# One half step of a windowed-attention transformer: its scores in one run, its value projections together at the end, the roots of the norms ahead of the softmax, and every softmax division on POOL

## The chip, the cores and the metric

The kernel runs on one core of a Trainium2 chip. The metric is the device time of one execution in microseconds (us). The engines are TensorE (PE in the profile; its weight loads are listed apart as PEld), VectorE (DVE), ScalarE (ACT), GpSimd (POOL) and SyncE (SP, which issues nearly all DMAs here). Each takes its instructions in the order in which they were written; semaphores tie the engines together.

## The reference, cut to what matters

The input is 16 sequences of 256 tokens with 128 features, all in float32. A first block adds one layer of causal attention. The second block, which takes most of the time and holds the whole change, runs six layers over the normed result. Cut to its core, with `x` of shape (16, 256, 128), 16 heads of 64 features, and windows of 32 tokens:

```python
def attn_layer(x, Wqkv, qs, ksc, Wo):
    q, k, v = split_heads(x @ Wqkv)            # 16 heads x 64
    q = l2norm(q) * qs                          # norm over the 64 features of a head
    k = l2norm(k) * ksc
    q = q * cos * scale + rotate_half(q) * sin * scale
    k = k * cos / scale + rotate_half(k) * sin / scale
    sim = einsum('bhwie,bhwje->bhwij', windows(q), look_back(windows(k))) * 8
    attn = softmax(where(mask, -max, sim))      # 32 queries x 64 keys (own window, one before)
    out = einsum('bhwij,bhwje->bhwie', attn, look_back(windows(v)))
    return merge_heads(out) @ Wo

for i in range(6):
    x = attn_layer(shift_tokens(x), Wqkv[i], q_scale[i], k_scale[i], Wo[i]) + x
    x = ffn_layer(shift_tokens(x), ln_g[i], ln_b[i], W1[i], b1[i], W2[i], b2[i]) + x
```

`shift_tokens` moves half of the features one token down. `ffn_layer` is a layer norm, two matrices of 128 x 341 with a gelu gate, and a matrix back.

## The kernel before, in words

The second block is a pipeline over `n`, which counts layer and sequence together (6 x 16 = 96 values). A step `n` has two halves, `half(n, 0)` and `half(n, 1)`. A half works at once on the scores of `n`, on the projections of `n + 2`, on the norms of `n + 1`, and on the values of the half before it: in `half(n, 0)` those of heads group `u = 1` of `n - 1`, in `half(n, 1)` those of `u = 0` of `n`. The gated feed-forward works on pairs of sequences, so that its pieces fall differently on even and odd `n`. Four kinds of half follow each other, 48 times: **A** is `half(even, 0)`, **B** `half(even, 1)`, **C** `half(odd, 0)`, **D** `half(odd, 1)`. In this text a half is counted from its first mask matmul, which is the last step but one of the written half before; the value projection that follows the masks (and, in C, the matmuls `w2` before it) is thus at the head of the counted half.

The order inside each half is written out by hand. A function `in_order` ties every instruction of PE, DVE, ACT and POOL to the one before it on its engine, so that these four run in the written order. SP's queue is not tied. The functions, in short, with their lines:

- `proj_qk` (L463 to L477): a group of q and k heads: matmuls into a PSUM tile `qk` (one for q, one for k); ACT squares it (L464); DVE multiplies it with the rotary tables into `t` (L465, 1024 elements wide, it waits for ACT on the same tile); POOL adds the squares (L474) and the two rotary products (L477, twice, into `tq`). A half does it for group i early, called `qk i` here, and for group j late, `qk j`, whose q part and k part stand apart on PE.
- `norms` (called by `sums`) and `roots`: matmuls sum the squares (L484), ACT copies them (L489), PE transposes them (`nT`, L495), and DVE makes the reciprocal roots with a shift trick and three Newton steps: L499, L503, then three times L506, L507, L508. POOL spreads the k part into `kb` (L511). Only halves A and C do this, for `n + 1`.
- `spread_k` and `norm_k`: PE transposes `kb` into PSUM (`bc`, L522), DVE scales the keys with it (L536), and eight DMAs per step move q and k into the layout of the scores (`us`, L538).
- `masks`, `sim`: the scores of one `u` on top of masks (L563, L583). One call of `sim` is one group of heads; a half makes four.
- `soften`: DVE scales the scores by the roots of q's norms (L595) and takes the row maximum (L603); POOL subtracts it (L604). Then `power` (exponential, ACT, L610) and, in the next half, `share`: DVE sums and inverts (L617, L618), and the division is a multiplication (L620).
- `attn_T`, `attn_v`, `project_out`: PE transposes the weights (`aT`, L626), ACT copies them (L628), PE multiplies them with v (`po`, L646), ACT copies (L655); in the next step the output matrix is applied (`wo`, L666), and DVE adds it to the residual (`yT`, L671).
- `proj_v`: two pieces, c = 0 and 1, each one matmul (L546), one ACT copy into `vn` (L552) and DMAs into `vs`, the copy of v that is shifted by one window: L553 for each piece, L555 for piece 0 alone.
- The feed-forward: `glu_center` (`cen`, L685), `glu_var` (`pv`, L696), `glu_norm` (`rs`, L708), `glu_part` (`hg` and `ha`, L728 and L729), `glu_out` (`w2`, L742).

PSUM has eight banks here: four for the scores and the value products (two tiles of two banks), and four for everything else, through `psum1`. So a `psum1` tile must wait until the last reader of the tile that held its bank before is done:

```python
ps_o = st.enter_context(tc.tile_pool(name="ps_o", bufs=4, space=PSUM))
ps_s = st.enter_context(tc.tile_pool(name="ps_s", bufs=2, space=PSUM))
```

Of the kernel before, what the change touches and what calls it, by code (L numbers as in the profile page):

```python
# [11 lines left out]
ALU = mybir.AluOpType  # L12
# [9 lines left out]
NG = HEADS // 4  # L22
# [16 lines left out]
def tile_transformer(  # L39
# [16 lines left out]
    nc = tc.nc  # L56
    P = 128
# [298 lines left out]
    with ExitStack() as st:  # L356
# [18 lines left out]
        def psum1(name):  # L375
            return ps_o.tile([P, 512], F32, tag="o", name=name)
# [115 lines left out]
        def roots(n, n2):  # L492
            ps = psum1(f"nT_{n}").rearrange("p (h g m) -> p h g m", h=4, g=4)
            for h in range(2):
                nc.tensor.transpose(  # L495
                    ps[:, h].rearrange("p g m -> p (g m)"), n2[:, h].rearrange("p a m -> p (a m)"), ident
                )
            x = p2.tile([P, 2, NG, 8], F32, tag="nx", name=f"nx_{n}")
            nc.vector.tensor_scalar(x, ps[:, 0:2, :, 0:8], 1e-24, None, ALU.max)  # L499

            y = p3.tile([P, 2, NG, 8], F32, tag="rn", name=f"rn_{n}")
            x_, y_ = (v.rearrange("p h g m -> p (h g m)") for v in (x, y))
            nc.vector.tensor_scalar(y_.bitcast(I32), x_.bitcast(I32), -0.5, 1597463007.0, ALU.mult, ALU.add)  # L503
            for _ in range(3):
                z = p4.tile([P, 64], F32, tag="nz", name=f"nz_{n}")
                nc.vector.tensor_tensor(z, x_, y_, ALU.mult)  # L506
                nc.vector.scalar_tensor_tensor(z, z, -0.5, y_, ALU.mult, ALU.mult)  # L507
                nc.vector.scalar_tensor_tensor(y_, z, 1.5, y_, ALU.add, ALU.mult)  # L508
            rn[n] = y
            kb = p1.tile([P, 2, NG, P], F32, tag="kb", name=f"kb_{n}")  # L510
            nc.gpsimd.tensor_copy(  # L511
                kb.rearrange("p h g (i d) -> p (h g) i d", d=32),
                y.rearrange("p h g m -> p (h g) m")[:, :, 4:8].unsqueeze(3).to_broadcast([P, 8, 4, 32]),
            )
            kbs[n] = kb
# [97 lines left out]
        def share(n, i):  # L613

            seg = exs[n, i].rearrange("p g (h k) -> p (g h) k", h=2)
            rec = p4.tile([P, 8], F32, tag="rec", name=f"rec_{n}_{i}")
            nc.vector.tensor_reduce(rec, seg, AX.X, ALU.add)  # L617
            nc.vector.reciprocal(rec, rec)  # L618
            on = nc.vector if i == 1 else nc.gpsimd
            on.tensor_tensor(seg, seg, rec.unsqueeze(2).to_broadcast([P, 8, 64]), ALU.mult)  # L620

        def attn_T(n, i):
            ex = exs.pop((n, i))
# [52 lines left out]
        def glu_shift(m):  # L676
            b = m % 8
            x2 = x2s[m] = p1.tile([P, 2 * S], F32, tag="gl", name=f"x2_{m}")
            for i in range(2):
                shifted(x2[:, i * S : (i + 1) * S], 2 * b + i)  # L680

        def glu_center(m):
            x2 = x2s.pop(m)
            ps = psum1(f"cen_{m}")
            nc.tensor.matmul(ps, center, x2, start=True, stop=True)  # L685
            sq2 = p1.tile([P, 2 * S], F32, tag="h1", name=f"fsq_{m}")
            nc.scalar.activation(sq2, ps, AF.Square)
            xc = p1.tile([P, 2 * S], F32, tag="h2", name=f"xc_{m}")
            nc.scalar.copy(xc, ps)
            xns[m] = sq2, xc  # L690
# [12 lines left out]
        def glu_norm(m):  # L703
            l = m // 8
            rstd, xc = xns[m]
            ps = psum1(f"rs_{m}")
            for t in range(4):
                nc.tensor.matmul(  # L708
                    ps[:, t * P : (t + 1) * P],
                    rstd[:, t : t + 1].to_broadcast([P, P]),  # L710
                    ident,
                    start=True,
                    stop=True,
                    is_transpose=True,
                )
            xn = p1.tile([P, 2 * S], F32, tag="xn", name=f"xn_{m}")
            nc.vector.tensor_tensor(xn, ps, xc, ALU.mult)
            nc.gpsimd.tensor_scalar(xn, xn, vecs[:, l, V_G : V_G + 1], vecs[:, l, V_B : V_B + 1], ALU.mult, ALU.add)
            xns[m] = xn

        def glu_part(mm, i):
            l = mm // 8
            if mm % 8 == 0 and i == 0:
                load_glu(l)
            xn = xns[mm]
            a, m = DI_PARTS[i]
            pg, ph = psum1(f"hg_{mm}_{i}"), psum1(f"ha_{mm}_{i}")
            nc.tensor.matmul(pg[:m], W["1"][:, DI + a : DI + a + m], xn, start=True, stop=True)  # L728
            nc.tensor.matmul(ph[:m], W["1"][:, a : a + m], xn, start=True, stop=True)  # L729
            g = p1.tile([P, 2 * S], F32, tag="gl", name=f"g_{mm}_{i}")  # L730
            nc.scalar.activation(g[:m], pg[:m], AF.Gelu, bias=vecs[:m, l, V_B1 + 3 + i : V_B1 + 4 + i])
            h = p1.tile([P, 2 * S], F32, tag=f"h{i}", name=f"h_{mm}_{i}")
            nc.vector.scalar_tensor_tensor(
                h[:m], ph[:m], vecs[:m, l, V_B1 + i : V_B1 + i + 1], g[:m], ALU.add, ALU.mult
            )
            hs[mm, i] = h
# [8 lines left out]
        def leave(s):  # L745

            ps = psum1(f"fin_{s}")
            for t in range(2):
                c0 = (s % 2) * S + t * P
                nc.tensor.transpose(ps[:, t * P : (t + 1) * P], yT[s // 2][:, c0 : c0 + P], ident)  # L750
            res = p2.tile([P, 2, E], F32, tag="res", name=f"res_{s}")
            nc.sync.dma_start(res, out[s].rearrange("(t p) e -> p t e", p=P))
            nc.vector.tensor_tensor(res, ps[:, :S].rearrange("p (t e) -> p t e", t=2), res, ALU.add)
            nc.sync.dma_start(out[s].rearrange("(t p) e -> p t e", p=P), res)
# [6 lines left out]
        def has(n):  # L761
            return 0 <= n < N

        def do(n, f, *a):
            if has(n):
                f(n, *a)

        n2s = {}
# [4 lines left out]
        def half(n, u):  # L773
            even = n % 2 == 0
            m = n // 2 - 1 if even else (n - 3) // 2
            glu = lambda m: 0 <= m < N // 2
            i, j = 2 * u, 2 * u + 1
            b, bu = (n, 0) if u else (n - 1, 1)
            bi, bj = 2 * bu, 2 * bu + 1
            do(b, share, bi)  # L780
            do(b, share, bj)
            do(n, sim, u, 0)
            do(n, sim, u, 1)
            for k in range(2):
                do(n + 2, proj_qk, i, k)
            if u == 0:
                do(n + 1, sums)
            else:
                do(n + 1, spread_k, 1)
                do(n + 1, norm_k, 1)  # L790
                if not even and glu(m):
                    glu_norm(m)
            do(n, sim, u, 2)
            do(n, sim, u, 3)
            do(n, soften, i)
            do(n, soften, j)
            do(n - 1, project_out, u)
            if u:
                do(n + 3, shift)
                if even and glu(m):  # L800
                    glu_shift(m)
            elif has(n + 1):
                roots(n + 1, n2s.pop(n + 1))
            do(b, attn_T, bi)
            do(b, attn_T, bj)
            do(n, proj_v, u, 0)
            do(b, attn_v, bi)
            if not even and u == 0 and glu(m):
                glu_center(m)
            do(n + 2, proj_qk, j, 0)  # L810
            if even and u == 0 and glu(m - 1):
                glu_part(m - 1, 2)
            if not even and glu(m):
                if u == 0:
                    glu_var(m)
                else:
                    glu_part(m, 0)
                    glu_part(m, 1)
            do(n + 2, proj_qk, j, 1)
            if u == 0:  # L820
                do(n + 1, spread_k, 0)
                do(n + 1, norm_k, 0)
            do(n, power, i)
            do(n, power, j)
            do(b, attn_v, bj)
            do(*((n, masks, 1) if u == 0 else (n + 1, masks, 0)))
            if even and u and glu(m - 1):
                glu_out(m - 1)
                if m - 1 >= (DEPTH - 1) * 8:
                    leave(2 * ((m - 1) % 8))  # L830
                    leave(2 * ((m - 1) % 8) + 1)
            do(n, proj_v, u, 1)

        last = {}
# [119 lines left out]
```

## Time and profile before

| what | value |
|---|---|
| time, median of 3 runs | 3670.28 us (3663.98 to 3673.59) |
| the profiled execution's own time | 3670.73 us |
| its span, first to last instruction | 3668.9 us |
| mean granted TensorE clock | 0.992 |
| busy: PE, DVE, POOL, ACT | 3511.4, 2822.9, 2538.0, 1890.9 us |
| halves of the pipeline | 4 kinds, 48 of each |
| division L620 | 288 on POOL, mean 1115 ns; 96 on DVE, mean 1111 ns |

The page of the profile gives the busy time of each engine, a chain of work that ended last, and groups of instructions by line with their mean time and with what ended the idle time in front of them. The timeline gives single instructions: the start in us, the time taken, engine, line, operation, the tiles written and read, and how many were merged into the row. Where an engine was idle in front of a row, the length and the releaser stand in brackets. A PE row's time runs to the modelled end of its last matmul, which overlaps the next row; the distance from start to start says what a row takes of PE.

### The profile page before, as it was taken

How to read it: one execution, taken by the hardware profiler on the slowest of the kernel's cores; microseconds unless marked ns; L12 is line 12 of the kernel's file. 1: busy time of each engine (PE TensorE's matmuls, PEld its weight loads, DVE VectorE, ACT ScalarE, POOL GpSimd, SP SyncE). 2: the span in 40 equal slices, each digit the busy share in tenths (PEclk: the TensorE clock that was granted, in tenths of full speed). 3: DMA queues.
4: the chain of work that ended last, by engine and by line, in shares of the span. 5: the costliest groups of instructions: out<-in, count | busy, mean ns of one | idle time of the engine just before them, and what ended most of it. 6: DMA issues, size and time to landing. Idle time of an engine off the chain costs nothing.

```text
span 3668.9 us, 153688 instructions
## 1 busy us (share of the span) xinstructions
PE 3511.4 (96%) x68032; PEld 2455.5 (67%) x68032; DVE 2822.9 (77%) x4882; ACT 1890.9 (52%) x3180; POOL 2538.0 (69%) x2667
## 2 busy tenths in 40 slices
PE   8888799999999999999999999999999999999998
PEld 6666566666666766766666666666666666666665
DVE  4454688887888887888887888877888887888784
ACT  4444345555555555555555555545555555555453
POOL 1000587877777778777777777777777777777772
PEclk9999899999999999999999999999999999999999
DMA  2000233333433334433334333334433343433332
GB/s 80 8 8 7 59 104 95 99 99 100 109 104 99 88 87 121 111 90 90 98 99 105 104 104 99 88 90 116 111 89 94 98 105 86 111 103 100 91 103 61
DMA packets 249445, 331.66 MB, mean 90 GB/s; under 512 B 74446, under 2 KB 105548, under 8 KB 247884
## 3 DMA queue, kind: packets, MB, share of 16 engines
q1 hardware_dynamic: 248060, 321.13, 32.8%
q8 instruction: 536, 8.78, 1.0%
q14 instruction: 129, 1.06, 0.1%
q10 hardware_dynamic: 720, 0.70, 0.1%
HBM read 28.12 MB, written 4.19 MB: 9 GB/s over the span
## 4 chain that ended last, share of the span: by engine, by line
PE 79%; DVE 11%; ACT 4%; issue 3%; POOL 2%; DMA 1%; SPq 0%; ACTq 0%; DVEq 0%; POOLq 0%
PE qk L463 17%; PE po L646 11%; PE v L546 9%; PE wo L666 8%; PE sim L583 6%; PE w L742 4%; PE hg L728 3%; PE ha L729 3%; PE aT L626 3%; PE n L484 2%; DVE tq L536 2%; PE bc L522 2%; DVE t L465 2%; PE sim L563 2%; PE st L222 1%
## 5 line engine op out<-in xcount | busy, mean ns | idle before, releaser
L465 DVE TENSOR_TENSOR t<-qk,ab 128x1024 f32<-128x1024 f32 x768 | 916.1, 1218 | 280.9 <-ACT sq L464 253.6
L477 POOL TENSOR_TENSOR tq<-t 128x512 f32<-128x512 f32 x768 | 961.2, 1273 | 85.3 <-DVE t L465 63.7
L463 PE MATMUL qk<-xs,wqk 128*128 128x256 f32 x3072 | 788.9, 392 | 1.7 <-DVE yT L671 1.5
L474 POOL TENSOR_TENSOR sq<-sq 128x512 f32<-128x512 f32 x384 | 488.2, 1271 | 277.8 <-ACT sq L464 268.1
L464 ACT ACTIVATE sq<-qk 128x512 f32<-128x512 f32 x768 | 459.3, 598 | 374.3 <-PE qk L463 365.2
L463 PEld LDWEIGHTS qk<-xs,wqk 128*128 128x128 f32 x3072 | 553.7, 190 | 146.7 <-issue 45.8
L628 ACT COPY aT<-aT 128x512 f32<-128x512 f32 x384 | 207.4, 586 | 599.7 <-PE aT L626 599.4
L646 PEld LDWEIGHTS po<-aT,vs 64*64 64x64 f32 x12288 | 327.7, 134 | 205.6 <-issue 110.7
L546 PE MATMUL v<-wv,xs 128*128 128x512 f32 x768 | 423.1, 633 | 27.7 <-ACT aT L628 21.2
L604 POOL TENSOR_TENSOR sm<-sm,mx 128x512 f32<-128x512 f32 x384 | 396.0, 1043 | 29.3 <-DVE mx L603 28.0
L646 PE MATMUL po<-aT,vs 64*64 64x32 f32 x12288 | 394.2, 222 | 9.7 <-issue 6.2
L583 PEld LDWEIGHTS sim<-us 64*32 64x32 f32 x24576 | 260.8, 105 | 205.6 <-issue 189.4
L646 PE MATMUL po<-aT,vn 64*64 64x32 f32 x12288 | 386.3, 219 | 2.1 <-issue 2.1
L552 ACT COPY vn<-v 128x512 f32<-128x512 f32 x384 | 225.0, 586 | 314.9 <-PE v L546 312.3
L666 PE MATMUL wo<-ao,wout 128*128 128x256 f32 x1536 | 383.2, 392 | 1.0 <-ACT ao L655 1.0
L620 POOL TENSOR_TENSOR ex<-ex,rec 128x512 f32<-128x512 f32 x288 | 317.1, 1115 | 43.9 <-ACT vn L552 20.3
L646 PEld LDWEIGHTS po<-aT,vn 64*64 64x64 f32 x12288 | 329.8, 135 | 2.3 <-issue 2.3
L583 PE MATMUL sim<-us 64*32 64x64 f32 (+1 forms) x24576 | 323.3, 221 | 3.1 <-DMA us<-tq 3.1
L666 PEld LDWEIGHTS wo<-ao,wout 128*128 128x128 f32 x1536 | 276.0, 189 | 49.7 <-ACT ao L655 1.7
L655 ACT COPY ao<-po 128x512 f32<-128x512 f32 x384 | 222.4, 579 | 116.7 <-PE po L646 116.7
L617 DVE TENSOR_REDUCE rec<-ex 128x8 f32<-128x512 f32 x384 | 252.1, 657 | 34.0 <-ACT ex L610 34.0
L603 DVE TENSOR_REDUCE mx<-sm 128x8 f32<-128x512 f32 x384 | 263.5, 686 | 13.3
(122 smaller groups left out, 5244.4 us busy)
## 6 DMA issues: line engine op xcount, KB each, us to landing
us<-tq SPq DMA_DIRECT2D x768, 256.0 KB, 3.9
vs<-vn SPq DMA_DIRECT2D x384, 192.0 KB, 4.1
vs<-vn SPq DMA_DIRECT2D x192, 64.0 KB, 2.8
wqk<-in_f_wqkv_dram SPq DMA_DIRECT2D x96, 64.0 KB, 2.8
ab<-in_tables_dram SPq DMA_DIRECT2D x6, 1024.0 KB
wv<-in_f_wqkv_dram SPq DMA_DIRECT2D x12, 256.0 KB, 4.6
wout<-in_f_wo_dram SPq DMA_DIRECT2D x24, 128.0 KB, 4.1
x<-in_x_dram SPq DMA_DIRECT2D x16, 128.0 KB, 2.7
```

Of the source, the lines that this page charges most:

```text
L463: nc.tensor.matmul(ps[:, t * S : t * S + S], W["qk", g][:, k, t, :], xs[n], start=True, stop=True)
L464: nc.scalar.activation(sq2[:, k].rearrange("p t n -> p (t n)"), ps, AF.Square)
L465: nc.vector.tensor_tensor(t12[:, k].rearrange("p f t n -> p f (t n)"), ps.unsqueeze(1).to_broadcast([P, 2, 2 * S]), W["ab", l][:, k].rearr ...
L474: nc.gpsimd.tensor_tensor(sq[n, g], sq2[:, :, 0, :], sq2[:, :, 1, :], ALU.add)
L477: nc.gpsimd.tensor_tensor(tq[n, g][:, t], t12[:, :, 0, t, :], t12[:, :, 1, 1 - t, :], ALU.add)
L546: nc.tensor.matmul(ps, xs[n][:, P * c : P * c + P], W["v"][:, u].rearrange("p g x d -> p (g x d)"), start=True, stop=True)
L583: nc.tensor.matmul(ps[WIN * r : WIN * r + WIN, x, col + first : col + 64], qk[part, g, 0, WIN * c : WIN * c + WIN], qk[part, g, 1, WIN * ( ...
L603: nc.vector.tensor_reduce(mx, seg, AX.X, ALU.max)
L604: nc.gpsimd.tensor_tensor(seg, seg, mx.unsqueeze(2).to_broadcast([P, 8, 64]), ALU.subtract)
L620: on.tensor_tensor(seg, seg, rec.unsqueeze(2).to_broadcast([P, 8, 64]), ALU.mult)
L646: nc.tensor.matmul(po[DH * y : DH * y + DH, h, x, g, WIN * r : WIN * r + WIN], v[64 * h : 64 * h + 64, r // 2, 2 * g + y, x, :], aT[64 * h ...
L666: nc.tensor.matmul(ps[:, :S].rearrange("p (h m) -> p h m", h=2), W["out"][:, g, 2 * u + x, :], a[:, x, :, g, :], start=(j == 0), stop=(j == 3)
```

## The change

Four moves, and nothing is computed differently:

- All four calls of `sim` stand together at the start of the half, ahead of the projection of group i. Before, two stood ahead of it and two behind it and behind the norms.
- `attn_T` and, in halves A and C, `roots` stand ahead of `soften` and `project_out`. Before, they came after them.
- `proj_v` of piece 0 moves from between `attn_T` and `attn_v` to the end of the half, next to piece 1.
- The division is always on POOL. Before, one in four (i = 1, in halves B and D) was on DVE.

```diff
@@ share
             nc.vector.reciprocal(rec, rec)
-            on = nc.vector if i == 1 else nc.gpsimd
-            on.tensor_tensor(seg, seg, rec.unsqueeze(2).to_broadcast([P, 8, 64]), ALU.mult)
+            nc.gpsimd.tensor_tensor(seg, seg, rec.unsqueeze(2).to_broadcast([P, 8, 64]), ALU.mult)
@@ half
             do(b, share, bi)
             do(b, share, bj)
-            do(n, sim, u, 0)
-            do(n, sim, u, 1)
+            for g in range(NG):
+                do(n, sim, u, g)
             for k in range(2):
                 do(n + 2, proj_qk, i, k)
             if u == 0:
...
                 do(n + 1, norm_k, 1)
                 if not even and glu(m):
                     glu_norm(m)
-            do(n, sim, u, 2)
-            do(n, sim, u, 3)
+            do(b, attn_T, bi)
+            do(b, attn_T, bj)
+            if u == 0 and has(n + 1):
+                roots(n + 1, n2s.pop(n + 1))
             do(n, soften, i)
             do(n, soften, j)
             do(n - 1, project_out, u)
@@
                 do(n + 3, shift)
                 if even and glu(m):
                     glu_shift(m)
-            elif has(n + 1):
-                roots(n + 1, n2s.pop(n + 1))
-            do(b, attn_T, bi)
-            do(b, attn_T, bj)
-            do(n, proj_v, u, 0)
             do(b, attn_v, bi)
...
                 if m - 1 >= (DEPTH - 1) * 8:
                     leave(2 * ((m - 1) % 8))
                     leave(2 * ((m - 1) % 8) + 1)
+            do(n, proj_v, u, 0)
             do(n, proj_v, u, 1)
```

Lines behind L619 move up: the transposes are L625 after the change, `wo` is L665, `yT` is L670.

## The prediction, made before the changed kernel ran

> **What bounds the kernel now.** I read the page first. PE is busy 96% of the span, and the chain that ended last is 79% PE:
>
> ```profile
> PE 3511.4 (96%) x68032; PEld 2455.5 (67%) x68032; DVE 2822.9 (77%) x4882; ACT 1890.9 (52%) x3180; POOL 2538.0 (69%) x2667
> PE 79%; DVE 11%; ACT 4%; issue 3%; POOL 2%; DMA 1%; SPq 0%; ACTq 0%; DVEq 0%; POOLq 0%
> ```
>
> Then PE's timeline, half by half. Half A of 2029.31 lasts to 2045.75, 16.44 us; B 13.41, C 19.14, D 16.88; these lengths recur with almost no spread. From start to start nothing is idle; only v waits, 0.24 us, for the copy of the transposed weights.
>
> ```profile
> 2031.47 1.99 PE L463 MATMUL qk<-xs,wqk 128*128 128x256 f32 x8
> 2033.40 1.07 PE L484 MATMUL n<-sq,cst 128*32 128x256 f32 x16
> 2037.21 1.04 PE L626 MATMUL aT<-cst,ex 128*128 128x128 f32 x8
> 2038.49 1.12 PE L546 MATMUL v<-wv,xs 128*128 128x512 f32 x2 [0.24 <-ACT aT L628]
> 2043.29 1.03 PE L463 MATMUL qk<-xs,wqk 128*128 128x256 f32 x4
> 2044.16 0.60 PE L522 MATMUL bc<-cst,kb 128*128 128x128 f32 x4
> ```
>
> So PE sets the time, and whatever makes it wait is added. The timelines of DVE and POOL for the same half show how close DVE follows:
>
> ```profile
> 2033.34 2.36 DVE L465 TENSOR_TENSOR t<-qk,ab 128x1024 f32<-128x1024 f32 x2 [0.70 <-ACT sq L464]
> 2035.61 0.68 DVE L595 TENSOR_TENSOR sm<-sim,rn 128x512 f32<-128x512 f32 x1
> 2038.25 0.41 DVE L671 TENSOR_TENSOR yT<-wo,yT 128x256 f32<-128x256 f32 x1
> 2038.83 0.75 DVE L503 TENSOR_SCALAR rn<-nx 128x64 int32<-128x64 int32 x1
> 2039.61 0.99 DVE L506 TENSOR_TENSOR nz<-nx,rn 128x64 f32<-128x64 f32 x1
> 2041.16 0.22 DVE L506 TENSOR_TENSOR nz<-nx,rn 128x64 f32<-128x64 f32 x1
> 2042.46 0.23 DVE L508 SCALAR_TENSOR_TENSOR rn<-nz,rn 128x64 f32<-128x64 f32 x1
> 2042.60 1.22 DVE L465 TENSOR_TENSOR t<-qk,ab 128x1024 f32<-128x1024 f32 x1
> ```
>
> ```profile
> 2036.03 2.50 POOL L477 TENSOR_TENSOR tq<-t 128x512 f32<-128x512 f32 x2
> 2038.48 2.04 POOL L604 TENSOR_TENSOR sm<-sm,mx 128x512 f32<-128x512 f32 x2
> ```
>
> Two things are to be seen. DVE has no idle time from 2033.34 until its product of qk j's q part ends at 2043.82; `bc`, which takes that tile's bank, starts on PE at 2044.16, 0.34 us later. And the small L503 and the first L506 take 0.75 and 0.99 us where later ones take 0.22: they end at 2039.58 and 2040.60, just as POOL's two subtractions (2038.48 to 2040.52) end. While POOL works on two SBUF tiles, these wait.
>
> [...] I go by the rows, which have no gap from start to start.
>
> **The change on PE alone.** T counts from the first mask matmul. Steps from start to start, from PE's rows: masks 0.34; a value piece 1.05 ahead of scores, 0.85 ahead of another piece (as `hg` to `ha`); all scores 1.54; qk i 1.92 ahead of the sums, 1.83 ahead of `bc`; sums 1.00; `aT` 0.87; `nT` 0.22; `wo` 1.92; `po` 1.06; qk j0 0.97; `hg`, `ha`, qk j1 0.86 each; `bc` and second `po` 1.59. In A: scores at 2.24, qk i at 3.78 (before 2.16), sums 5.70, `aT` 6.70, `nT` 7.57, `wo` 7.79, `po` 9.71, qk j0 10.77, qk j1 13.46, `bc` 14.32, end 15.91. B, C and D by the same steps: 12.95, 18.71, 16.77. Together 64.34 against 65.87: without waits the change saves 1.53 us per four halves, mainly v's wait for the copy and the joined pieces.
>
> **What DVE makes of it, A and C.** Qk i starts 1.62 us later in the half, while DVE still owes the same list before qk j: two products, roots, two softmax scalings, `yT`, one product. From a qk's start to its first product is 1.87 us (2031.47 to 2033.34), so in A the two products run 5.64 to 8.00. Their end starts POOL's two L477 at 8.08, 1.25 each, to 10.58. The roots, now next on DVE, need L499 (0.21) first, so L503 meets the first L477 and L506 the second, as they met the subtractions. From the second POOL operation's end to the last L508's end was 2.17 us (2040.52 to 2042.69): roots end at 12.75. From L595's start to `yT`'s end is 3.05 (2035.61 to 2038.66): `yT` is written at 15.72.
>
> The built programs' banks say who waits. After the change qk j1 takes the bank of `wo`, whose reader is `yT`; before, it took that of v. PE reaches qk j1 at 13.64 (0.18 of it a wait of `wo` for the copy of `aT`) and starts at 15.78. DVE's product of qk j0 ends at 16.86, so `bc` starts at 16.92 and the half ends at 18.51. **A: +2.07.** Behind PE's wait stand `bc`, the second `po` and the next half; the maxima and subtractions come some 5 us later, yet the exponentials still end where they did, behind ACT's table load.
>
> In C, `w2` (2.68) shifts all: qk i at 6.46, products to 10.68, L477 10.76 to 13.26, roots to 15.43, `yT` to 18.40. Here `bc` takes `wo`'s bank: reached at 17.30, it starts at 18.46, end 20.05. **C: +0.91.**
>
> **Transposes, B and D.** Both divisions are now on POOL, 2 x 1.04: in B to about 4.9, in D to 6.6; the 0.92 to 1.29 that DVE saves lies in its idle time. In B `aT` of i starts at 6.14, but `aT` of j takes the bank of qk i's q part, read until 6.86: it starts at 6.92 instead of 6.57. The copy of the first `aT` starts 0.63 after it (2037.21 to 2037.85) and takes 0.58, so `wo`, in its bank, starts at 7.41; end 13.37. **B: -0.04.** In D the first `aT` waits for that product, 6.92 instead of 6.49, and the second has the same bank as the first: it waits for ACT's copy, 8.13, and starts at 8.19. `wo` at 8.62 instead of 7.36, end 18.03. **D: +1.15.**
>
> **The rest.** POOL in B is 0.9 us longer and ends its next division in C at 8.2; C's `aT` needs it at 9.8: hidden; uncovered, 1 us per C. In SP's queue the pieces of v now stand as three issues behind four of `us`, each 0.55 to 1.0. In B: `us` from 0.95 to 3.9, the last L553 at 5.3, and with the median landing of 4.1 it is there at 9.4; `po` asks for it at 9.57.
>
> ```profile
> vs<-vn SPq DMA_DIRECT2D x384, 192.0 KB, 4.1
> L553 SPq DMA_DIRECT2D vs<-vn x384: 511/562/1682, 447.1 to 3634.1; - x192
> DMA to landing us min/median/max: 2.4/4.1/7.0
> ```
>
> Bounds are 0 at the median and 2.7 at the largest landing; I take 0.2, near the median row. In D there is about 0.9 us of slack, in A and C more.
>
> **Sum.** 2.07 - 0.04 + 0.91 + 1.15 = 4.09 per four halves, times 48 is 196, with 48 x 0.2 = 10 for the DMAs 206. The profiled execution took 3670.73 us (span 3668.9, median 3670.28, so no correction): 3877 us.
>
> **Rivals.**
> - *The roots go unblocked.* If DVE got through ahead of POOL, they would take 2.85 us (eleven operations at about 0.26). A would end at 16.59, C at 18.89: 0.15 - 0.04 - 0.25 + 1.15 = 1.01, times 48 is 48: 3719. If only one of the two blocks, A ends at 17.28 and C at 18.89: 82, so 3752. For it: the order of two starts 0.1 us apart decides. Against: POOL is released by the same product that DVE has to end first.
> - *Faster: PE's steps alone count.* The one long run of scores and the joined pieces bring their 1.53 x 48 = 73: 3597. It needs `yT` by 13.6 in A, 2.1 us earlier than my sum; it decides there. For it: PE is the bound and loses v's wait. Against: DVE's list had only 0.34 us of slack before.
> - *The pieces of v land late.* With 7.0 us, `po` in B waits 2.7: 130 us, less the 10 counted, 3997; in half of the steps 3937. For it: seven issues in a row, where L553's landings vary; against: `po` waits for `vs` only four times, 5.0 us in all, in the trace of before.
> - *The change does nothing.* The built order differs in every half, so only a cancellation would give 3671.
>
> **How the numbers follow.** Forecast 0.77, unblocked or half-blocked roots 0.09, late pieces 0.07, faster 0.05, no change 0.02. The range reaches from half-blocked roots to late pieces in half of the steps, 3750 to 3945. About 0.3% (11 us) is what can be told from no change; only the faster case lies below that, so faster 0.05, same 0.02, slower 0.93.
>
> **What would show it.** PE's busy share should fall to about 91%. In A: a wait of PE of about 2 us for DVE's `yT` (L670) ahead of qk j1; in C one of about 1.2 us ahead of `bc`; in D the second `aT` waiting 0.8 us for ACT. L503's mean should rise from 0.61 to about 1.2 us and L506's from 0.48 to about 0.55, both ending with L477. If halves A and C are as long as before, the DVE chain is wrong; if D is, the bank; if B is longer, look at `vs`.

## The result and the profile after

The changed kernel takes **3933.2 us** (median of 4 runs, 3927.96 to 3938.95) against 3667.77 us of the kernel before (4 runs, 3663.98 to 3673.59): ratio 1.0723, 95% interval 1.07 to 1.0745, slower by some 265 us. The profiled execution took 3935.57 us, its span 3933.8. The forecast was 3877, with a range of 3750 to 3945.

The page first, the lines that answer to those shown of before:

```profile
PE 3595.4 (91%) x68032; PEld 2487.1 (63%) x68032; DVE 2789.2 (71%) x4786; ACT 1911.0 (49%) x3180; POOL 2629.9 (67%) x2763
PE 56%; DVE 23%; issue 4%; ACT 3%; POOL 1%; DMA 1%; SPq 0%; DVEq 0%; ACTq 0%; POOLq 0%
```

PE's share falls to 91% as said, and DVE's part of the chain doubles from 11% to 23%, although DVE has less to do. But PE's busy time also rises, from 3511.4 to 3595.4 us, with the same 68032 instructions. No step of the prediction does that.

PE's timeline in a half A from 2016.14 to 2034.61 (18.47 us), the rows around the wait:

```profile
2019.78 1.99 PE L463 MATMUL qk<-xs,wqk 128*128 128x256 f32 x8
...
2031.77 1.13 PE L463 MATMUL qk<-xs,wqk 128*128 128x256 f32 x4 [1.89 <-DVE yT L670]
2032.99 0.63 PE L522 MATMUL bc<-cst,kb 128*128 128x128 f32 x4
```

DVE's and POOL's timelines in the same half:

```profile
2021.65 2.36 DVE L465 TENSOR_TENSOR t<-qk,ab 128x1024 f32<-128x1024 f32 x2 [2.19 <-ACT sq L464]
...
2024.32 1.09 DVE L503 TENSOR_SCALAR rn<-nx 128x64 int32<-128x64 int32 x1
2025.44 1.22 DVE L506 TENSOR_TENSOR nz<-nx,rn 128x64 f32<-128x64 f32 x1
...
2028.51 0.23 DVE L508 SCALAR_TENSOR_TENSOR rn<-nz,rn 128x64 f32<-128x64 f32 x1
...
2031.30 0.41 DVE L670 TENSOR_TENSOR yT<-wo,yT 128x256 f32<-128x256 f32 x1
```

```profile
2024.09 2.50 POOL L477 TENSOR_TENSOR tq<-t 128x512 f32<-128x512 f32 x2 [0.32 <-DVE t L465]
```

This is the chain that the prediction walked. POOL's two sums run from 2024.09 to 2026.59; L503 ends 0.05 us after the first of them and the first L506 0.08 us after the second (from the times before rounding). The roots end at 12.60 in the half (12.75 was said), `yT` at 15.57 (15.72), qk j1 starts at 15.63 (15.78), `bc` at 16.85 (16.92).

The profile's list of PE's waits puts totals to it. Each row names who waited for whom, then the sum in us, how often, and the longest:

```profile
PE qk L463 <- DVE yT L670: 91.3, 45, 3.1
PE bc L522 <- DVE yT L670: 48.2, 46, 1.1
PE aT L625 <- DVE t L465: 47.4, 97, 1.6
PE aT L625 <- ACT aT L627: 35.3, 46, 0.8
...
PE po L645 <- DMA vs<-vn: 9.6, 9, 2.2
```

The first row is A, the second C, the next two the transposes (55 of the 83 us in D, 20 in B), the last the pieces of v. Together 232 us; 265 are lost.

The rest is in the clock. The trace's clock records show TensorE at half speed for 61.2 us (13 records) in before and for 232.1 us (39 records) after. Windows of the changed kernel, three around the end of one half A (1943.11 to 1962.83, 19.72 us) and two around the same place in the quiet half A shown above; columns: stretch, length, busy time of PE, PEld, DVE, ACT, POOL, granted clock, DMA share, GB/s:

```profile
1956.05:1959.46 3.41, 1.53 (x5) 0.68 (x4) 3.34 (x6) 1.76 (x2) 2.90 (x3) 1.00 0.02 5
1959.46:1962.87 3.41, 3.41 (x78) 2.55 (x76) 3.08 (x5) 2.68 (x4) 2.04 (x3) 0.50 0.02 5
1962.87:1966.29 3.42, 3.42 (x16) 1.26 (x12) 1.89 (x5) 1.40 (x3) 3.42 (x4) 0.50 0.68 174
2027.73:2031.14 3.41, 2.15 (x6) 0.64 (x5) 3.23 (x8) 2.58 (x4) 2.03 (x2) 1.00 0.00 0
2031.14:2034.55 3.41, 2.69 (x72) 2.10 (x72) 3.34 (x5) 1.60 (x2) 2.03 (x3) 1.00 0.00 0
```

Both halves have the same wait of 1.9 us. In the first it lies whole in one stretch, in which PE works for 1.53 of 3.41 us, and the two stretches that follow run at half the clock. In the second a boundary cuts the wait into 1.26 and 0.63 us, and nothing happens. The stretches aren't chosen freely: every half-clock record of a trace starts and ends on one grid of 3.413 us (the last, cut off where the trace ends, apart). Of the 47 halves A behind the first, which is still in the start-up and is left out here and below, 21 end in such a record. Five of the 21 stand at the start of a layer, where A is 2.6 us longer without any record too (in e2 below). In the other 16, A and B together take 34.6 us, and 32.1 where no record follows (mean of 24): 2.5 us each time.

In the table, "undisturbed" is the median of the halves without a half-clock record and, for B, without a wait for v (with these waits it is 13.52); the mean is over the 44 halves in the middle of the run.

| half | before, median | predicted | after, undisturbed | after, mean |
|---|---|---|---|---|
| A | 16.44 | 18.51 | 18.47 | 19.35 |
| B | 13.41 | 13.37 | 13.39 | 14.21 |
| C | 19.15 | 20.05 | 20.08 | 20.36 |
| D | 16.89 | 18.03 | 18.27 | 18.40 |

### The profile page after: what moved, and what is told of

It is laid out like the page before. It is cut to its first block, busy times and chain, and to the rows that moved or that the text cites. A ratio compares the mean times of both kernels' runs of the same rounds, so it can differ in the third digit from the quotient of the medians.

```text
span 3933.8 us, 153471 instructions
## 1 busy us (share of the span) xinstructions
PE 3595.4 (91%) x68032; PEld 2487.1 (63%) x68032; DVE 2789.2 (71%) x4786; ACT 1911.0 (49%) x3180; POOL 2629.9 (67%) x2763
## 4 chain that ended last, share of the span: by engine, by line
PE 56%; DVE 23%; issue 4%; ACT 3%; POOL 1%; DMA 1%; SPq 0%; DVEq 0%; ACTq 0%; POOLq 0%
PE qk L463 12%; PE v L546 10%; PE po L645 8%; PE sim L583 7%; DVE t L465 6%; DVE nz L506 4%; PE wo L665 4%; PE w L741 3%; PE aT L625 3%; DVE sm L595 3%; DVE rn L503 3%; ACT sq L464 2%; PE hg L727 2%; PE ha L728 2%; PE sim L563 2%
## 5 line engine op out<-in xcount | busy, mean ns | idle before, releaser
L463 PE MATMUL qk<-xs,wqk 128*128 128x256 f32 x3072 | 797.9, 395 | 91.5 <-DVE yT L670 91.3
L645 PEld LDWEIGHTS po<-aT,vs 64*64 64x64 f32 x12288 | 341.2, 140 | 129.7 <-issue 100.8
L645 PE MATMUL po<-aT,vs 64*64 64x32 f32 x12288 | 411.8, 227 | 10.8 <-DMA vs<-vn 9.6
L619 POOL TENSOR_TENSOR ex<-ex,rec 128x512 f32<-128x512 f32 x384 | 392.1, 1041 | 21.3 <-ACT vn L552 12.3
L645 PE MATMUL po<-aT,vn 64*64 64x32 f32 x12288 | 403.6, 224 | 0.0
L665 PE MATMUL wo<-ao,wout 128*128 128x256 f32 x1536 | 372.5, 385 | 1.7
L645 PEld LDWEIGHTS po<-aT,vn 64*64 64x64 f32 x12288 | 344.4, 141 | 0.0
L665 PEld LDWEIGHTS wo<-ao,wout 128*128 128x128 f32 x1536 | 276.4, 190 | 52.7 <-ACT aT L627 22.4
L625 PE MATMUL aT<-cst,ex 128*128 128x128 f32 x1536 | 225.8, 279 | 86.2 <-DVE t L465 47.4
L583 PE MATMUL sim<-us 64*32 64x64 f32 (+1 forms) x24576 | 298.5, 223 | 5.5 <-DMA us<-tq 5.5
L627 ACT COPY aT<-aT 128x512 f32<-128x512 f32 x384 | 216.8, 587 | 172.9 <-PE aT L625 172.7
```

What stands on the lines that cost most here:

```text
L463: nc.tensor.matmul(ps[:, t * S : t * S + S], W["qk", g][:, k, t, :], xs[n], start=True, stop=True)
L583: nc.tensor.matmul(ps[WIN * r : WIN * r + WIN, x, col + first : col + 64], qk[part, g, 0, WIN * c : WIN * c + WIN], qk[part, g, 1, WIN * ( ...
L619: nc.gpsimd.tensor_tensor(seg, seg, rec.unsqueeze(2).to_broadcast([P, 8, 64]), ALU.mult)
L625: nc.tensor.transpose(ps[:, g, :], ex[:, g], ident)
L645: nc.tensor.matmul(po[DH * y : DH * y + DH, h, x, g, WIN * r : WIN * r + WIN], v[64 * h : 64 * h + 64, r // 2, 2 * g + y, x, :], aT[64 * h ...
L665: nc.tensor.matmul(ps[:, :S].rearrange("p (h m) -> p h m", h=2), W["out"][:, g, 2 * u + x, :], a[:, x, :, g, :], start=(j == 0), stop=(j == 3)
```

## Experiments

The theory: A and C are set by DVE's chain, which the later qk i and the roots' waiting for POOL (L503 takes 1108 ns in the mean, 614 in before) have lengthened; D by banks; and the waits bring the half clock on top. Rivals: the division on POOL, the later pieces of v, the new place of the roots or transposes by itself.

**e1: the division alone put back.**

```diff
-            nc.gpsimd.tensor_tensor(seg, seg, rec.unsqueeze(2).to_broadcast([P, 8, 64]), ALU.mult)
+            on = nc.vector if i == 1 else nc.gpsimd
+            on.tensor_tensor(seg, seg, rec.unsqueeze(2).to_broadcast([P, 8, 64]), ALU.mult)
```

> The changed kernel with the old division (i = 1 on DVE). Theory 1 (DVE's list and the PSUM banks make PE wait in A, C and D, and the long wait in A lets the TensorE clock drop to half): the divisions end 1 to 3 us before their transposes, so nothing moves: 3933 us, within 12. Theory 2 (divisions on POOL hold the transposes in B and D): up to one division, 1.04 us, comes back in each of B and D: 3833.

Measured: 3931.77 us (ratio to before 1.071, 1.0694 to 1.0726). The division costs nothing that can be seen, on either engine.

**e2: PE's wait in A filled with repeated work.** The last `ha` of half A is computed three times, 1.7 us more.

```diff
-            nc.tensor.matmul(ph[:m], W["1"][:, a : a + m], xn, start=True, stop=True)
+            for _ in range(3 if i == 2 else 1):
+                nc.tensor.matmul(ph[:m], W["1"][:, a : a + m], xn, start=True, stop=True)
```

> The changed kernel with the last ha of the feed-forward computed three times instead of once in half A (the same values are written again), 1.7 us more of PE work inside the 2 us in which PE waits for yT. Theory 1: the extra work costs nothing on the path, PE does not go idle, and the clock stays full: the 170 us more at half clock than before the change vanish, about 60 us of time with them: 3870. Theory 3 (the clock drops for another reason, such as the small matmuls of the long run of scores): the clock stays as it is, 3933. Theory 4 (PE's own work is the bound in A too): 48 x 1.7 = 82 us more, 4015.

Measured: 3891.15 us (1.0599, 1.0581 to 1.0616). More work, and 42 us less. A's undisturbed length stays at 18.47; the records at A's end go from 21 to none, B's mean from 14.21 to 13.59. C keeps its wait, and shows nine. So the half clock is a cost of its own. The gain is 42 us, 21 less than was expected: 21 records at 2.5 us are 52, and C and D are longer here by 0.08 and 0.18 us in the mean, 12 us in 44 halves.

**e3: the roots alone put back behind `project_out`.**

```diff
-            if u == 0 and has(n + 1):
-                roots(n + 1, n2s.pop(n + 1))
             do(n, soften, i)
...
+            elif has(n + 1):
+                roots(n + 1, n2s.pop(n + 1))
             do(b, attn_v, bi)
```

> The changed kernel with the roots alone put back behind project_out; the transposes of the weights stay ahead. Theory 1: in A yT is no longer behind the roots, but the product of qk j0, which bc waits for, still is, and the roots then meet POOL's two subtractions: bc at 15.8 instead of 16.8, A 1.06 us shorter, C unchanged because kb comes later: 51 us, and perhaps part of the 60 us of slow clock: 3820 to 3882. A theory in which the roots' place does not matter: 3933.

Measured: 3882.11 us (1.0578, 1.0559 to 1.0596), at the slow end of what was expected. PE no longer waits for `yT`, but `bc` waits for POOL's `kb`: 155 us in all, where after had 7. A shrinks to 17.51, C grows to 20.23. The wait has changed its name; the order of the roots is a fifth of the loss.

**e4: POOL's two rotary sums of group i behind the spreading of `kb`, in A and C.** The roots stay where the change put them; POOL stands idle while DVE makes them.

```diff
-                for t in range(2):
-                    nc.gpsimd.tensor_tensor(tq[n, g][:, t], ...)
+                if g:
+                    turn(n, g)          # the two sums, as before, for group j
...
                 roots(n + 1, n2s.pop(n + 1))
+            if u == 0:
+                do(n + 2, turn, 0)      # and for group i, here
```

> The changed kernel with POOL's two rotary sums of group i (halves A and C) written behind kb, so that POOL is idle while DVE makes the roots. Theory 1 with the blocking: L503 and the first L506 fall to about 0.25 us, the roots take 2.85 instead of 4.7 us, yT and bc come 1.9 us earlier; A loses its wait (1.95 us less), C 1.2 us: 150 us, and the slow clock goes with the wait: 3720 to 3785. Theory 5 (these two operations are slow by themselves): their means stay at 1.1 and 0.55 us, and the time at 3933.

Measured: 3719.09 us (1.0133, 1.0118 to 1.0148). The same two POOL instructions in each A and C, only later, give back 214 of 265 us. It is also what the first rival put on unblocked roots, 3719. The groups of L503 and L506 (L507 and L510 in this kernel, four lines were added), first after, then e4; busy time in all, and the mean in ns:

```profile
L506 DVE TENSOR_TENSOR nz<-nx,rn 128x64 f32<-128x64 f32 x288 | 158.6, 551 | 10.1 <-DVE rn L503 0.2
L503 DVE TENSOR_SCALAR rn<-nx 128x64 int32<-128x64 int32 x96 | 106.4, 1108 | 3.3
```

```profile
L510 DVE TENSOR_TENSOR nz<-nx,rn 128x64 f32<-128x64 f32 x288 | 64.8, 225 | 10.0 <-DVE rn L507 0.2
L507 DVE TENSOR_SCALAR rn<-nx 128x64 int32<-128x64 int32 x96 | 18.7, 195 | 3.3
```

1108 against 195 ns, and 551 against 225: what lies between is waiting for POOL, 181 us of DVE's busy time. The half-clock time is back to 57.8 us, A to 16.57, C to 18.84, B is at 13.56. D stays at 18.21, 1.33 us above before: 64 us in 48 halves, more than the 51 us that e4 still loses.

**e5: value piece 0 alone put back** between `attn_T` and `attn_v`.

```diff
+            do(n, proj_v, u, 0)
             do(b, attn_v, bi)
...
-            do(n, proj_v, u, 0)
             do(n, proj_v, u, 1)
```

> After, with the value piece 0 alone put back between attn_T and attn_v. Group i's projection then starts 0.86 us earlier in every half, and with it the whole chain of VectorE. Theory 1 (VectorE's chain ahead of qk j1 and bc sets A and C, and TensorE's clock falls to half after waits of about 2 us): A's wait ahead of qk j1 falls from 2.0 to about 1.1 us and A shortens by 0.9; C, whose qk j1 now has wo's bank, by 0.15; B loses 0.2 (the piece waits for the copy of aT); D stays at 18.3. That is 0.85 x 48 = 41, and with the shorter wait the clock records at half speed should become rare in A, some 30 to 60 us more: 3830 to 3860. Theory 2 (the clock does not depend on the length of this wait): 3892. Theory 3 (the place of the value piece is free): 3933.

Measured: 3898.46 us (1.0625, 1.0601 to 1.0648). A shortens as said, to 17.60, and the records at its end nearly vanish. But now some 20 appear in C, although PE waits as long there as in A (1.07 and 1.02 us in the median), and the expected gain is missed by 38 us. PE's rows in a half C, ahead of a record from 2196.73 to 2200.14:

```profile
2194.43 1.04 PE L695 MATMUL pv<-cst,fsq 128*128 128x1 f32 x8
2196.54 1.93 PE L463 MATMUL qk<-xs,wqk 128*128 128x256 f32 x4 [1.07 <-DVE yT L670]
```

In front of C's wait stand the matmuls of `pv`, which move one column each. If they are no work, C lacks 2.1 us (2194.43 to 2196.54), as much as A in the changed kernel.

That reading was then counted out in the traces of all fourteen kernels, in every window with a recorded full clock. A grid window "lacks" the time in which no matmul record runs, `pv` counted as none:

| lacking in a full-clock window of 3.413 us | windows | followed by one at half clock |
|---|---|---|
| under 1.2 us | 14369 | 4 |
| 1.2 to 1.7 | 318 | 60 |
| 1.7 to 1.9 | 98 | 68 |
| over 1.9 | 188 | 178 |

With `pv` counted as work, 64 windows at half clock follow one that lacks under 1.2 us, instead of 4; 23 of the 64 are those of C in e5. (The first ten traces gave the rule, with the same shares; the two runs that follow were told from it beforehand.)

**e9: half of e2's filling,** so that a wait of 1.2 us is left in A.

```diff
-            for _ in range(3 if i == 2 else 1):
+            for _ in range(2 if i == 2 else 1):
```

> After, with the last matmuls ha of half A done twice instead of once (in e2 three times): 0.86 us of repeated work in TensorE's wait of 2.05 us ahead of qk j1, so that 1.2 us of it are left. Theory W (the clock is set on a fixed grid of 3.413 us: a window in which TensorE lacks work for more than about 1.8 us is followed by one at half speed; under 1.2 us never): no window of A holds more than about 1.7 us of wait, half-clock records at A's end all but vanish although a wait of 1.2 us stays; the time is that of e2, 3891, within 8 us. Rival (what counts is that there is a wait at all, or its sum): records fall in proportion, about 3912. Rival 2 (the repeated work costs its own time): 3960 and more.

Measured: 3902.3 us (1.0637, 1.0621 to 1.0653), 3 us outside what the rule allowed. The records at A's end fall from 21 to 2, where a fall in proportion would leave 12, though more than half of the wait remains (52.6 of 91.3 us): its share in one window decides, not that it is there. The time alone settles less: it lies 11 us above e2's, the rival's 3912 lies 10 us above it, and the profiled executions of e2 and e9 are 2.4 us apart.

**e10: e5, with real columns ahead of `pv` in C:** two repeated matmuls into a part of the tile that nothing reads.

```diff
+            for _ in range(2):
+                nc.tensor.matmul(pv[:, 8:488], center, sq2[:, :480], start=True, stop=True)
             for t in range(4):
                 nc.tensor.matmul(pv[:, t : t + 1], sq2[:, t * P : (t + 1) * P], mean1, ...)
```

> e5 (value piece 0 put back) with two repeated matmuls of 480 columns ahead of glu_var's matmuls in half C, written to a part of pv that nothing reads. In e5, A and C have the same wait of 1.2 us for yT ahead of qk j1; A has 3 half-clock records behind it and C some 20, and in C glu_var's 0.9 us of matmuls with one column each stand ahead of the wait. Theory W counts these as no work: 2.1 us together. With 0.9 us of matmuls put there, C keeps its length of 20.0 in the undisturbed case and the records of C vanish: its mean falls from 20.96 to 20.0 to 20.2 and D's from 18.77 to 18.2 to 18.3; 1.2 to 1.5 us times 48 is 58 to 73 less than e5's 3898: 3825 to 3845. Rival (C's records come from the waits of D or of transfers): 3898, or 3940 if the repeated matmuls are paid.

Measured: 3859.67 us (1.0525, 1.0505 to 1.0545), 39 us below e5. That is above the range of 3825 to 3845. C's records go to none, its mean from 20.96 to 20.54 and D's from 18.77 to 18.45. The two matmuls take 1.70 us and not 0.9, so the undisturbed C grows from 19.96 to 20.35; without these 0.39 x 48 = 19 us it would be 3841, inside the range. The fill leaves no wait for `yT` in C either, so e10 alone can't tell `pv` from the wait; e5's A does, which has the same wait, no `pv` and hardly a record.

**e6: before, with the scores in one run.** Nothing else is changed.

```diff
-            do(n, sim, u, 0)
-            do(n, sim, u, 1)
+            for g in range(NG):
+                do(n, sim, u, g)
...
-            do(n, sim, u, 2)
-            do(n, sim, u, 3)
```

> Before, with all four calls of sim in one run ahead of qk i and nothing else changed. Theory 1 (VectorE follows TensorE with 0.34 us of slack in A, so a later qk i is paid): qk i starts 0.8 us later; A +0.5, C +0.2, D up to +0.6, B 0: 3705 to 3735. Rival (one run of scores only saves a change between kinds of matmul): 0.1 us per half, 192 halves, about 3650. The roots stand where they stood, so L503 and L506 should keep 0.61 and 0.48 us.

Measured: 3736.88 us (1.0184, 1.0169 to 1.0199), 2 us above what was expected. By medians A +0.22, C +0.12, D +0.86: in D `wo` now waits for the product of qk i, which comes later (15.6 us of such waits in all, none in before). There the step from `rs` to what follows it grows from 0.53 to 0.94 us, and that from the transposes to v from 0.87 to 1.28. L503 and L506 take 0.52 and 0.48 us in the mean, hardly other than in before.

**e7: before, with `attn_T` ahead of `project_out`.**

```diff
+            do(b, attn_T, bi)
+            do(b, attn_T, bj)
             do(n - 1, project_out, u)
...
-            do(b, attn_T, bi)
-            do(b, attn_T, bj)
             do(n, proj_v, u, 0)
```

> Before, with attn_T alone put ahead of project_out; the roots, scores, value pieces and divisions stay. Theory 1: TensorE's wait of v for the copy of the transposed weights (0.24 us per half in before) is covered by wo; in D the second aT gains a wait of about 0.4 us for the product of qk i's k part, whose bank it takes, and in B wo one of up to 0.3. Sum -0.24 x 4 + 0.4 + 0.2 = about -0.35 per four halves, 3645 to 3660. Rival (early transposes are the loss of the whole change): 3700 and more, with D at 18 us.

Measured: 3663.87 us (0.9989, 0.998 to 0.9999), 4 us above what was expected, and far from the rival. The transposes ahead aren't the loss. D pays 0.44 (its `aT` takes 1.33 us up to `wo` instead of 0.87 up to v, as was expected of the bank), B 0.10; C gains 0.51, A 0.17.

**e8: after, with three edits:** e4's and e5's, and `attn_T` behind `project_out` in B and D.

```diff
-            do(b, attn_T, bi)
-            do(b, attn_T, bj)
+            if u == 0:
+                do(b, attn_T, bi)
+                do(b, attn_T, bj)
...
             do(n - 1, project_out, u)
+            if u:
+                do(b, attn_T, bi)
+                do(b, attn_T, bj)
```

> After, with three edits together: POOL's two rotary sums of group i behind the spreading of kb in A and C (as in e4), value piece 0 back between attn_T and attn_v, and attn_T behind project_out in B and D only. Theory 1 by its parts: A 16.2 (no wait for yT is left), B 13.3, C 18.7, D 17.1 (wo waits 0.4 us for the product of qk i; the two aT have banks of their own): 65.3 against 65.89 of before, times 48 is 28 less: 3640, between 3620 and 3665. Rival (D's loss is not the bank of aT but the time at which its weights are divided): D stays at 18.2, and the time at 3690 to 3700.

Measured: 3682.1 us (1.0037, 1.0024 to 1.005): between the two, nearer to the rival. A, B and C come as said (16.04, 13.30, 18.74), but D is 17.88 instead of 17.1. `wo` waits 0.34 us for the product, as counted, but v waits again for the copy of `aT`, and the scores of D take 1.63 us where 1.54 was meant, 2.4 at worst; 14.3 us of the waits in front of them are put down to issue. Why they are slower when they come 0.86 us earlier isn't settled.

**e11: e7 in A and C only.** The edit is e8's `if u == 0` and `if u`, in the kernel before.

> Before, with attn_T ahead of project_out in A and C only; in B and D it stays behind. From the half lengths of e7: A 16.27 and C 18.64 as there, B 13.41 and D 16.89 as in before: 65.21 against 65.89, times 48 is 33 less: 3635, between 3625 and 3648. Rival (the gain of A and C is given back in the halves behind them, as B and D are released later): 3660 to 3668.

Measured: **3626.77 us** (0.9887, 0.9872 to 0.9902): 44 us under the kernel before, the best of all. A 16.29, C 18.64, D 16.87 as said, and B shortens too, to 13.02, which was not foreseen: in before, v waits there for DVE's scaling of the keys (L536, 32 times), and the step from `aT` to v falls from 1.21 us to 0.87. The page's first line:

```profile
PE 3487.0 (96%) x68032; PEld 2444.6 (67%) x68032; DVE 2823.1 (78%) x4882; ACT 1894.2 (52%) x3180; POOL 2541.9 (70%) x2667
```

**e12: e11 with the roots ahead of `soften`, and e4's order on POOL.**

> e11, with the roots ahead of soften in A and C as well, and POOL's two rotary sums of group i behind kb there (as in e4). Theory 1: in e7 bc of A still waits 0.35 us for kb; with the roots 2 to 3 us earlier, and not behind POOL (L503 0.19, L506 0.22 us), that goes: A 15.9, the others as in e11: 17 less than e11, 3618, between 3605 and 3635. Rival (the later scaling and yT then hold something, as in after): A 16.6 as in e4, 3650 and more.

Measured: 3628.75 us (0.9891, 0.9873 to 0.9909), the same as e11. A shortens to 15.89 as said, `bc`'s wait for `kb` goes from 24.0 us in all to 2.3, and B gives 0.4 back, 13.42: v there waits for DVE's scaling of the keys again (L540 in this kernel), 40 times and up to 0.6 us, and from `aT` to v it is 1.21 us as in before. What A saves, B gives back, probably because DVE's work did not shrink with PE's.

## Why the prediction was right, and where it fell short

- **A, C and B: right to within 0.04 us** against undisturbed halves. The waits came where they were said and lengthened the halves by as much: the third of PE's time in which no weights are loaded (PEld is busy for 67% of the span in before, for 63% in after) did not hide them. That L503 and L506 wait for POOL, argued from two rows of before, is shown by e4, where moving POOL's work alone brings their means from 1108 and 551 ns to 195 and 225.
- **D: mis-sized.** +1.15 was forecast, +1.38 came. PE's rows of one D, which starts at 1997.90:

```profile
2004.97 0.63 PE L625 MATMUL aT<-cst,ex 128*128 128x128 f32 x4 [0.43 <-DVE t L465]
2006.37 0.63 PE L625 MATMUL aT<-cst,ex 128*128 128x128 f32 x4 [0.77 <-ACT aT L627]
2006.83 1.89 PE L665 MATMUL wo<-ao,wout 128*128 128x256 f32 x8
```

  Both waits are there, in the order said. The first transpose starts at 7.07 and not 6.92, the second at 8.47 and not 8.19. DVE's product begins 1.93 us behind qk i, not 1.87, and from the end of an engine's work to PE's next start 0.14 to 0.15 us pass (ACT's copy ends at 2006.23), where the walk had used 0.06.
- **The pieces of v: right.** PE's matmuls wait 9.6 us for them against 2.6 in before, 7 more; 10 were said. (The prediction's 5.0 us of before is from a list that counts the weight loads too; there it is now 20.8.)
- **Missing: the clock.** The four halves give 2.03 - 0.02 + 0.93 + 1.38 = 4.32, times 48 is 207, with 7 for the pieces 214, where the sum had 206. The other 51 of 265 had no term. The prediction asked only how long PE waits, and priced the work behind a wait as if its speed were given. e2 gives back 42 us with the waits of A filled; the 21 halves at 2.5 us make 52. That the range held the time is luck: its upper end comes from the late pieces, a cause that did not come about.
- **The rivals.** Unblocked roots did not happen. Their price, 3719, is what e4 measured, but the terms fit less well than the sum: A +0.13, B +0.15, C -0.31 and D +1.33, where +0.15, -0.04, -0.25 and +1.15 stood. For "PE's steps alone", DVE had to bring `yT` 2 us sooner; it didn't. The late pieces of v weren't late.

What the change is made of: the roots' wait for POOL and PE's wait behind it, with the clock, 214 us (e4). The 51 us that e4 still loses are another 51 than the clock's, and stand in D. Joined scores explain more than all of them (e6, 69 us by itself), and the early transposes give a little back in A and C (e7, e11). The division is free (e1). Part costs don't add up, since each removed wait uncovers another: e3 and e5 bring 51 and 35 us, although e4 shows that over 200 hang on the same chain.

## What to carry to other kernels

Before small operations are moved ahead on VectorE, look at what GpSimd will be doing at that very time: an engine's order can be right and its neighbour's wrong, and deferring two GpSimd instructions in every second half was worth 214 us here. A wait of TensorE is not priced by its length alone: where it filled more than half of a 3.413 us window, the next 3.4 or 6.8 us mostly ran at half the clock here (behind 246 of the 286 windows that lack over 1.7 us; of the changed kernel's 39 records 10 last 3.41 us and 27 last 6.83), so spread waits, or put work into them (e2, 42 us). Of a change in many parts, try each alone; here the one good part (transposes early in A and C) was hidden under the others.

## What the runs showed of the hardware that was not expected

- **The clock falls for waits of 2 us.** By the table above, a window of 3.413 us that lacks over 1.9 us of matmul work is followed by one at half clock in 178 of 188 cases, one that lacks under 1.2 us in 4 of 14369. Matmuls that move one column are taken as none in this (e5, where C has some 20 records and A 3); as work, they would make the 4 into 64. In the changed kernel a gap of 1.9 us did it where it fell whole into one window (1956.05 to 1959.46), and did not where a boundary cut it into 1.26 and 0.63 us (at 2031.14).
- **Adding 1.7 us of useless matmuls to every half A made the kernel 42 us faster** (e2).
- **One operation of VectorE on 64 numbers per partition (L503, SBUF to SBUF) takes 1.1 us beside POOL and 0.195 us without** (e4). In the changed kernel L503 ends 0.05 us after the first of POOL's two sums and the first L506 0.08 us after the second, both in 94 of the 96 halves A and C. Not every operation waits: the row maximum L603, which reads one SBUF tile, takes 0.69 us in the changed kernel, both where one of POOL's tensor operations covers it wholly (50 times) and where none runs (98 times).
